# DFTs with real and imaginary parts on the two halves of the partitions, in a kernel that hides them under a selective scan

## The chip, the cores and the metric

The kernel runs on one core of a Trainium2 chip. The core has five engines that run side by side: TensorE (PE, matrix products; its weight loads are listed apart as PEld), VectorE (DVE), ScalarE (ACT), GpSimd (POOL) and SyncE (SP, which issues the DMAs here). The metric is device time in microseconds (us), lower is better. A run is one execution; times before and after are medians of runs.

## The reference, cut to what matters

The input is `x`, four images of 64 x 64 pixels with 96 channels, in float32. Four layers follow one another for each image:

1. A group normalisation and a selective-scan block ("L0": projection, 3 x 3 depthwise convolution, scan in four directions over 4096 tokens, layer norm, gate, output projection), added to `x`. The result is `x0`.
2. A second selective-scan block ("L1") between two Fourier transforms. This is the layer that the change is in:

```
xf  = rfft2(x, axes=(1, 2), norm='ortho')          # 64 x 33 complex values per channel
x1  = stack([xf.real, xf.imag]) -> (64, 33, 192)   # the block works on 192 real channels
att = ss2d(x1)                                     # scan in four directions over 2112 tokens
out = x + irfft2(att[..., 0] + 1j * att[..., 1], s=(64, 64), norm='ortho')
```

3. and 4. Twice linear attention and a feed-forward net with values rounded to 8 bits, on 4096 tokens.

The transforms are small matrix products. Over the width, 64 real values give 33 complex ones; over the height, 64 complex values give 64 complex ones. A complex product over the height is `Re = C*re + S*im`, `Im = C*im - S*re`, so each output sums over a real and an imaginary input.

## The kernel before, in words

**The scan sets the frame.** `scans` (from line 473) runs 1728 steps in order. A step is one group of 4 of the 16 state values, for 128 channels, over one segment of 512, 384 or 320 tokens. Its core is four scans on VectorE (`hx`, `hy`, line 643) and one product on VectorE (`hcy`, line 807, once in each step), with TensorE transposing the inputs into PSUM (line 613) and the outputs back (line 665), ScalarE computing exponentials (line 618), and GpSimd two products (lines 636 and 789). Steps 0 to 767 are the scan of L0 (two phases of 384, two images each). Steps 768 to 1727 are the scan of L1 (four phases of 240, one image each).

**Everything else is side work, cut into pieces.** `fourier`, `project`, `gate`, `gated`, `inverse` and `tokens` are Python generators. Each `yield` ends a piece. A step has three places where at most one piece is put (`slot`, line 723). A place first adds `rate / 3` to an account `due`, and if `due` is 1 or more, a piece is written there and 1 is taken off:

```
due = min(due + st.z.ph.rate / 3, 3.0)
if due >= 1.0:
    due -= E.step(kind)
```

`RATES` (line 26) has one rate per phase: 1.75, 2.3, and four times 2.47 pieces per step. The order on TensorE, VectorE, ScalarE and GpSimd is exactly the order in which the program writes its instructions (`manual_schedule`, line 703), so a piece's matmuls stand between two groups of the scan's transposes and delay those behind them. The DMAs on SP are ordered by the framework's scheduler. A piece that evacuates PSUM can be put off to the next piece (`E.defer`). Within the scan, side work has one PSUM bank (tag `ms`), so a piece that wants the bank waits for the copy out of it.

**The order of the side work.** In phase 1 (steps 384 to 767): the end of L0 for the first pair, then `begin1` for images 0 and 1. `begin1` is `fourier`, then `project` and `gate`. In phase 2: the end of L0 for the second pair, `begin1` for images 2 and 3. Then `end1` for images 0, 1 and 2: `gated` (norm, gate and output projection), `inverse`, `tokens`. What is left when the steps are over runs at once (`E.finish`, line 813). After that `end1` of image 3 runs with nothing beside it, with eight PSUM banks: the tail.

**`fourier` (line 926)** works per image in two stages. The first is over the width: for each of 96 channels, weights `xw[:, :, i]` (64 partitions of width, 64 columns of height, read with a stride of 12 values) and moving operand `fw` (64 x 66: 33 real and 33 imaginary outputs) give `pz` (64 partitions x 66); six channels make a piece and a copy into `z` (line 956). The second is over the height: for each of the 33 frequencies two accumulating matmuls (lines 964 and 965), weights 64 x 96, moving 64 x 128, into `pfx`. By its yields it has 2 + 16 + 17 + 1 = 36 pieces.

**`inverse` (line 981)** also has two stages, for three groups of 32 channels. The first, over the height: for each channel two accumulating matmuls (lines 1001 and 1002), weights `a[:, :, r, i]` (64 partitions x 33 columns, read with a stride of 64 values), moving `ih[:, r]` (64 x 128), into `piv` (33 partitions x 128). Four channels fill a bank, and ScalarE copies it into `v` (line 1005). The second, over the width: for each block of 16 rows of the image two accumulating matmuls (line 1015), weights 33 x 64, moving 33 x 512, into `pio`; VectorE adds the image's `x` (line 1020), and SP stores it. By its yields it has 3 x (2 + 16 + 8) + 1 = 79 pieces.

A float32 matmul appears in the profile as two weight loads and two matmul records. "Record" below means one of these.

## Time and profile before

| what | value |
|---|---|
| median of 3 runs | 12443.53 us (12440.8 to 12446.42) |
| the profiled execution's own time | 12459.57 us |
| its span, first to last instruction | 12457.8 us |
| busy share PE / DVE / ACT / POOL | 79% / 85% / 73% / 71% |
| mean granted TensorE clock | 0.855 |
| steps 384 to 767 (two `fourier`) | 2857.6 to 5533.5 us |
| steps 768 to 1007 (two `fourier`) | 5533.5 to 7073.9 us |
| steps 1008 to 1247 / 1248 to 1487 / 1488 to 1727 | to 8586.9 / 10266.4 / 11891.2 us |
| the three `inverse` beside the scan, first to last matmul | 8227.0 to 8451.3, 9614.5 to 9877.4, 11019.6 to 11269.2 us |
| `inverse` in the tail | 12109.0 to 12235.1 us |

The stretches of the steps are read from the ends of the 1728 executions of line 807. A busy share is an average over stages that have different limits, so the table's shares say little about the transforms; the stretches in which they run have to be read on their own. A "granted clock" of 1.0 is TensorE at full speed, 0.5 at half.

### The profile page before, as it was taken

What the parts mean: (1) busy time and instruction counts of PE and PEld (TensorE: products, weight loads), DVE (VectorE), ACT (ScalarE), POOL (GpSimd) and SP (SyncE); (2) the same over time, 40 slices, a digit from 0 to 9 for tenths busy, and PEclk for the clock granted to TensorE, in tenths of its full rate; (3) what the DMA queues carried; (4) which work ended last, traced back from release to release, by engine and by line L of the source; (5) the groups of instructions that cost most, each with busy time, mean ns of one, the idle gap of its engine ahead of it and who ended that gap; (6) DMA issues with size and microseconds to landing.
All of it is one profiled execution on the core that took longest, in us unless ns stands there. A gap on an engine that the chain in (4) does not pass through costs nothing. (4 is left out here: it accounts for less than half of the span.)

```text
span 12457.8 us, 164218 instructions
## 1 busy us (share of the span) xinstructions
PE 9802.9 (79%) x54392; PEld 6990.4 (56%) x54392; DVE 10588.5 (85%) x10207; ACT 9116.3 (73%) x18615; POOL 8861.4 (71%) x7061
## 2 busy tenths in 40 slices
PE   6677777787788878878888787897778977887766
PEld 3455555456666556556665655665555555665544
DVE  6899999899889989988888889978988699888933
ACT  3678888897778888886677777767776577767723
POOL 2888898887778888886677788866667466675610
PEclk8789999888889989988789899888888688887875
DMA  4454444555554454455443534542244322532231
GB/s 143 119 135 120 116 119 114 145 155 151 143 129 125 119 136 130 118 153 145 136 113 114 137 113 133 150 107 93 76 132 118 80 87 79 155 102 83 82 87 25
DMA packets 1269534, 1468.97 MB, mean 118 GB/s; under 512 B 495491, under 2 KB 1032911, under 8 KB 1259207
## 3 DMA queue, kind: packets, MB, share of 16 engines
q1 hardware_dynamic: 1268679, 1458.47, 42.7%
q8 instruction: 427, 7.00, 0.2%
q14 instruction: 428, 3.51, 0.1%
HBM read 1221.67 MB, written 236.50 MB: 117 GB/s over the span
## 5 line engine op out<-in xcount | busy, mean ns | idle before, releaser
L636 POOL TENSOR_TENSOR hy_l<-du_l,bc_l 128x512 f32<-128x512 f32 (+2 forms) x3456 | 3955.3, 1165 | 2487.9 <-DVE hcy_l L807 1256.0
L789 POOL TENSOR_TENSOR hcx_l<-hx_l,bc_l 128x1024 f32<-128x1024 f32 (+2 forms) x1619 | 3527.7, 2179 | 331.8 <-DVE hx_l L643 285.7
L593 ACT ACTIVATE bx_l<-dut_l,bt_l 128x192 f32<-128x192 f32 (+2 forms) x6272 | 2772.0, 498 | 0.1
L665 PE MATMUL acc_l<-ident,hcy_l 128*128 128x128 f32 (+1 forms) x12012 | 1855.4, 303 | 400.5 <-DVE hcy_l L807 397.0
L665 PE MATMUL acc_l<-ident,hcx_l 128*128 128x128 f32 (+1 forms) x12018 | 1899.0, 307 | 330.2 <-POOL hcx_l L789 326.2
L618 ACT ACTIVATE ax_l<-delta_l,l_alog 128x512 f32<-128x512 f32 (+2 forms) x3456 | 2139.2, 667 | 0.0
L665 PEld LDWEIGHTS acc_l<-ident,hcy_l 128*128 128x128 f32 (+1 forms) x12012 | 1547.3, 155 | 968.1 <-DVE hcy_l L807 586.3
L643 DVE TENSOR_TENSOR_SCAN hx_l<-ax_l,state_l,b_l 128x512 f32<-128x512 f32 (+2 forms) x1653 | 1790.7, 1123 | 277.7 <-PE b_l L613 186.1
L665 PEld LDWEIGHTS acc_l<-ident,hcx_l 128*128 128x128 f32 (+1 forms) x12018 | 1557.5, 157 | 819.2 <-POOL hcx_l L789 577.2
L807 DVE TENSOR_TENSOR hcy_l<-hy_l,bc_l 128x1024 f32<-128x1024 f32 (+2 forms) x1618 | 1950.5, 1205 | 43.2
L643 DVE TENSOR_TENSOR_SCAN hy_l<-b_l,state_l,hy_l 128x512 f32<-128x512 f32 (+2 forms) x1653 | 1793.3, 1119 | 135.0 <-ACT b_l L618 114.5
L618 ACT ACTIVATE b_l<-delta_l,l_alog 128x512 f32<-128x512 f32 (+2 forms) x1917 | 1202.9, 628 | 876.7 <-DVE hx_l L643 831.4
L613 PE MATMUL b_l<-ident,bx_l 128*128 128x128 f32 (+1 forms) x6733 | 1207.2, 309 | 382.9 <-DVE hy_l L643 186.8
L618 ACT ACTIVATE ab_l<-delta_l,l_alog 128x512 f32<-128x512 f32 x1321 | 909.1, 688 | 687.2 <-DVE hx_l L643 655.6
L613 PEld LDWEIGHTS b_l<-ident,bx_l 128*128 128x128 f32 (+1 forms) x6733 | 851.0, 156 | 891.4 <-DVE hy_l L643 283.1
L643 DVE TENSOR_TENSOR_SCAN hx_l<-ax_l,state_l,ab_l 128x512 f32<-128x512 f32 x962 | 1177.0, 1264 | 132.5 <-PE ab_l L613 85.6
L643 DVE TENSOR_TENSOR_SCAN hy_l<-ab_l,state_l,hy_l 128x512 f32<-128x512 f32 x961 | 1176.2, 1258 | 98.1 <-ACT ab_l L618 63.7
L613 PE MATMUL ab_l<-ident,bx_l 128*128 128x128 f32 x5288 | 901.3, 306 | 436.0 <-DVE hy_l L643 219.7
L613 PEld LDWEIGHTS ab_l<-ident,bx_l 128*128 128x128 f32 x5288 | 655.1, 155 | 786.1 <-DVE hy_l L643 294.1
L656 POOL COPY state_l<-hx_l 128x2 f32<-128x2 f32 x1344 | 1077.6, 802 | 0.0
L272 PE MATMUL pc_l<-pad_l,l_dg 128*128 128x512 f32 (+2 forms) x1656 | 796.4, 569 | 80.1 <-ACT uh_l L250 71.8
L176 PE MATMUL pi_l<-xi_l,l_wi 96*128 96x384 f32 (+6 forms) x912 | 467.3, 628 | 266.3 <-DMA xi_l<-xn 97.8
(196 smaller groups left out, 12661.2 us busy)
## 6 DMA issues: line engine op xcount, KB each, us to landing
bc_l<-l_xd_l SPq DMA_DIRECT2D x1536, 256.0 KB
bc_l<-l_xd_l SPq DMA_DIRECT2D x384, 512.0 KB
bc_l<-l_xd_l SPq DMA_DIRECT2D x384, 384.0 KB
us_l<-l_u SPq DMA_DIRECT2D x96, 768.0 KB
l_y<-y_l SPq DMA_DIRECT2D x288, 256.0 KB
bc_l<-l_xd_l SPq DMA_DIRECT2D x192, 320.0 KB
yt_l<-l_y SPq DMA_DIRECT2D x264, 192.0 KB
yt_l<-l_y SPq DMA_DIRECT2D x128, 384.0 KB
```

The lines of the kernel that those rows point to most:

```text
L176: self.nc.tensor.matmul(out[i * cfg.PI : (i + 1) * cfg.PI, :n], wi[:, ki, half, :], xin[:, max(i, ki), :n], start=(ki == 0), stop=(ki == c ...
L272: nc.tensor.matmul(pc[:, : n * 64].rearrange("p (r w) -> p r w", w=64), diag[:, t, :], pad[:, r - p0 + dy : r - p0 + dy + n, dx : dx + 64] ...
L593: nc.scalar.activation(t[:n, b, :, ch], z.dut[:n, b, :, ch], AF.Copy, scale=z.bt[:n, b, m : m + 1])
L613: nc.tensor.transpose(pb[:, t : t + n], st.z.bx[st.q, j][:n, b, st.c], ident[:n, :n])
L618: nc.scalar.activation(out, z.delta[:, st.c, : z.S], AF.Exp, scale=z.blk.A[:, st.c, z.k, n : n + 1])
L636: nc.gpsimd.tensor_tensor(st.hy[:, j, :S], st.z.du[:, st.c, :S], st.z.b[st.q][:, j, :S], ALU.mult)
L643: nc.vector.tensor_tensor_scan(h[:, j, : z.S][:, ::step], a[:, : z.S][:, ::step], b[:, : z.S][:, ::step], 0.0 if z.first else z.state[st.c ...
L656: copy(z.state[st.c][:, n0 : n0 + 2].rearrange("p (j o) -> p j o", o=1), h[:, :, e : e + 1])
L665: nc.tensor.matmul(z.acc[st.c][:n, b, :], hc[:, j, t : t + n], ident, start=(n0 + j == 0 and b == 0), stop=(n0 + j == NST - 1 and b == 0), ...
L789: nc.gpsimd.tensor_tensor(hcx[:, :, :S], hx[:, :, :S], z.c[q][0][:, :, :S], ALU.mult)
L807: nc.vector.tensor_tensor(hcy[:, :, :S], st.hy[:, :, :S], z.c[q][1][:, :, :S], ALU.mult)
```

## The change

In `fourier`, `fw` and `fh` are laid out anew: real outputs of the first stage land on partitions 0 to 63 of `pz`, imaginary ones on 64 to 127. For that each channel has two matmuls (real, imaginary) with the same weights and 33 moving columns each, in place of one with 66. The copy takes 12 channels at once. The second stage then sums over 128 partitions in one matmul per frequency. In `inverse`, the real and imaginary parts of the attention output are loaded onto the two halves of the partitions, padded from 33 to 64 columns with zeros (a GpSimd memset), one group of channels ahead (`bufs=2`). The first stage has two matmuls per channel (real and imaginary output, onto the two halves of the partitions of `piv`), which share their weights and have 64 moving columns each; eight channels fill a bank. The second stage has one matmul per block of 16 rows, summing over all 128 partitions; two blocks go to the two halves of the partitions of one bank, and one VectorE instruction adds `x` for both. `fourier` now has 28 pieces and `inverse` 45. The rates go from 2.3 and 2.47 to 2.25 and 2.35. The constants are rearranged to match.

```diff
@@ -23,7 +23,7 @@
 SM = 512
 LATE, BURST = "late", "burst"
-RATES = [1.75, 2.3, 2.47, 2.47, 2.47, 2.47]
+RATES = [1.75, 2.25, 2.35, 2.35, 2.35, 2.35]
 EXP_LN = "natural_log_exp_and_others"
@@ -926,16 +926,17 @@
 def fourier(E, cst, x, b, dram, out):
     nc = E.nc
     xf = dram.tile([CH, 2, WF * HH], F32, name=f"xf_{b}", tag="xf", bufs=NB)
     out["xf"] = xf
     G = 12
     with E.pool(f"ff{b}") as sp:
-        fw = sp.tile([WW, 2 * WF], F32, name=f"fw_{b}", tag="fw")
+        fw = sp.tile([WW, 2, WF], F32, name=f"fw_{b}", tag="fw")
         nc.sync.dma_start(out=fw, in_=cst["fw"])
-        fh = sp.tile([HH, 2, 2 * HH], F32, name=f"fh_{b}", tag="fh")
+        fh = sp.tile([2 * HH, 2 * HH], F32, name=f"fh_{b}", tag="fh")
         nc.sync.dma_start(out=fh, in_=cst["fh"])
-        z = sp.tile([HH, 2 * WF, CH], F32, name=f"z_{b}", tag="z")
+        z = sp.tile([2 * HH, WF, CH], F32, name=f"z_{b}", tag="z")
         def load(c0):
             t = sp.tile([WW, HH, G], F32, name=f"xw_{b}_{c0}", tag="xw", bufs=2)
@@ -947,24 +948,24 @@
         yield
         for c0 in range(0, CH, G):
             xw, nxt = nxt, load(c0 + G) if c0 + G < CH else None
-            for i0 in range(0, G, 6):
-                pz = E.psum(f"pfz_{b}_{c0}_{i0}")[:HH, : 12 * WF].rearrange("p (c k) -> p c k", c=6)
-                for i in range(6):
-                    nc.tensor.matmul(pz[:, i, :], xw[:, :, i0 + i], fw, start=True, stop=True)
-                c1 = c0 + i0
-                E.defer(
-                    lambda c1=c1, pz=pz: nc.scalar.copy(z[:, :, c1 : c1 + 6], pz.rearrange("p c k -> p k c"))
-                )
-                yield
+            pz = E.psum(f"pfz_{b}_{c0}")[:, : G * WF].rearrange("p (c k) -> p c k", c=G)
+            for i in range(G):
+                for r in range(2):
+                    nc.tensor.matmul(
+                        pz[r * HH : (r + 1) * HH, i, :], xw[:, :, i], fw[:, r, :], start=True, stop=True
+                    )
+                if i == G // 2 - 1:
+                    yield
+            E.defer(
+                lambda c0=c0, pz=pz: nc.scalar.copy(z[:, :, c0 : c0 + G], pz.rearrange("p c k -> p k c"))
+            )
+            yield
         for k0 in range(0, WF, 4):
             nk = min(4, WF - k0)
             px = E.psum(f"pfx_{b}_{k0}").rearrange("p (k r h) -> p k r h", k=4, r=2)
             for i in range(nk):
                 o = px[:CH, i, :, :].rearrange("p r h -> p (r h)")
-                nc.tensor.matmul(o, z[:, k0 + i, :], fh[:, 0, :], start=True, stop=False)
-                nc.tensor.matmul(o, z[:, WF + k0 + i, :], fh[:, 1, :], start=False, stop=True)
-                if i == 1 and nk > 2:
-                    yield
+                nc.tensor.matmul(o, z[:, k0 + i, :], fh, start=True, stop=True)
             def put(k0=k0, nk=nk, px=px):
                 xo = sp.tile([CH, 2, 4, HH], F32, name=f"xo_{b}_{k0}", tag="xo", bufs=2)
@@ -980,47 +981,57 @@
 def inverse(E, cst, att, x, b, x1):
     nc = E.nc
-    G = 32
+    G, HC, WP = 32, 16, 64
+    xs, xd = (t.rearrange("(h w) c -> w h c", w=WW) for t in (x, x1))
     with E.pool(f"fi{b}") as sp:
-        ih = sp.tile([HH, 2, 2 * HH], F32, name=f"ih_{b}", tag="ih")
+        ih = sp.tile([2 * HH, 2, HH], F32, name=f"ih_{b}", tag="ih")
         nc.sync.dma_start(out=ih, in_=cst["ih"])
-        iw = sp.tile([WF, 2, WW], F32, name=f"iw_{b}", tag="iw")
+        iw = sp.tile([2 * WP, WW], F32, name=f"iw_{b}", tag="iw")
         nc.sync.dma_start(out=iw, in_=cst["iw"])
+        def load(c0):
+            a = sp.tile([2 * HH, WP, G], F32, name=f"at_{b}_{c0}", tag="at", bufs=2)
+            nc.gpsimd.memset(a[:, WF:, :], 0.0)
+            for r in range(2):
+                nc.sync.dma_start(
+                    out=a[r * HH : (r + 1) * HH, :WF, :], in_=att[:, :, r * CH + c0 : r * CH + c0 + G]
+                )
+            return a
+        nxt = load(0)
+        yield
+        yield
         for c0 in range(0, CH, G):
-            a = sp.tile([HH, WF, 2, G], F32, name=f"at_{b}_{c0}", tag="at")
-            for r in range(2):
-                nc.sync.dma_start(out=a[:, :, r, :], in_=att[:, :, r * CH + c0 : r * CH + c0 + G])
-            yield
-            yield
-            v = sp.tile([WF, G, 2, HH], F32, name=f"v_{b}_{c0}", tag="v")
-            for i0 in range(0, G, 4):
-                pv = E.psum(f"piv_{b}_{c0}_{i0}").rearrange("p (c r h) -> p c r h", c=4, r=2)
-                for i in range(4):
-                    o = pv[:WF, i, :, :].rearrange("p r h -> p (r h)")
-                    nc.tensor.matmul(o, a[:, :, 0, i0 + i], ih[:, 0, :], start=True, stop=False)
-                    nc.tensor.matmul(o, a[:, :, 1, i0 + i], ih[:, 1, :], start=False, stop=True)
-                    if i == 1:
+            a, nxt = nxt, load(c0 + G) if c0 + G < CH else None
+            v = sp.tile([2 * WP, G, HH], F32, name=f"v_{b}_{c0}", tag="v")
+            for i0 in range(0, G, 8):
+                pv = E.psum(f"piv_{b}_{c0}_{i0}").rearrange("p (c h) -> p c h", c=8)
+                for i in range(8):
+                    for r in range(2):
+                        nc.tensor.matmul(
+                            pv[r * WP : (r + 1) * WP, i, :], a[:, :, i0 + i], ih[:, r, :], start=True, stop=True
+                        )
+                    if i == 3:
                         yield
-                E.defer(lambda i0=i0, pv=pv, v=v: nc.scalar.copy(v[:, i0 : i0 + 4], pv[:WF]))
+                E.defer(lambda i0=i0, pv=pv, v=v: nc.scalar.copy(v[:, i0 : i0 + 8], pv))
                 yield
-            HC = 16
-            for h0 in range(0, HH, HC):
-                xr = sp.tile([WW, HC, G], F32, name=f"xr1_{b}_{c0}_{h0}", tag="xr", bufs=2)
-                nc.sync.dma_start(
-                    out=xr, in_=x.rearrange("(h w) c -> w h c", w=WW)[:, h0 : h0 + HC, c0 : c0 + G]
-                )
-                po = E.psum(f"pio_{b}_{c0}_{h0}").rearrange("p (h c) -> p h c", h=HC)[:WW]
-                for r in range(2):
-                    nc.tensor.matmul(
-                        po, iw[:, r, :], v[:, :, r, h0 : h0 + HC].rearrange("p c h -> p h c"),
-                        start=(r == 0), stop=(r == 1),
-                    )
-                    yield
+            for h0 in range(0, HH, 2 * HC):
+                xr = sp.tile([2 * WW, HC, G], F32, name=f"xr1_{b}_{c0}_{h0}", tag="xr", bufs=2)
+                po = E.psum(f"pio_{b}_{c0}_{h0}").rearrange("p (h c) -> p h c", h=HC)
+                halves = [
+                    (slice(k * WW, (k + 1) * WW), slice(h0 + k * HC, h0 + (k + 1) * HC)) for k in range(2)
+                ]
+                for p, h in halves:
+                    nc.sync.dma_start(out=xr[p], in_=xs[:, h, c0 : c0 + G])
+                for p, h in halves:
+                    nc.tensor.matmul(po[p], iw, v[:, :, h].rearrange("p c h -> p h c"), start=True, stop=True)
+                    yield
+                yield
                 nc.vector.tensor_tensor(xr, xr, po, ALU.add)
-                nc.sync.dma_start(
-                    out=x1.rearrange("(h w) c -> w h c", w=WW)[:, h0 : h0 + HC, c0 : c0 + G], in_=xr
-                )
+                for p, h in halves:
+                    nc.sync.dma_start(out=xd[:, h, c0 : c0 + G], in_=xr[p])
         yield
@@ -1292,10 +1303,10 @@
         "ident": np.eye(128),
         "group": (g[:, None] // 3 == g[None, :] // 3) / 3.0,
         "head_mask": (g[:, None] // 16 == g[None, :] // 16) * 16**-0.5,
-        "fw": np.concatenate([cw, -sw], 1) * rw,
-        "fh": np.stack([np.concatenate([ch, -sh], 1), np.concatenate([sh, ch], 1)], 1) * rh,
-        "ih": np.stack([np.concatenate([ch, sh], 1), np.concatenate([-sh, ch], 1)], 1) * rh,
-        "iw": np.stack([cw.T * fold, -sw.T * fold], 1) * rw,
+        "fw": np.stack([cw, -sw], 1) * rw,
+        "fh": np.block([[ch, -sh], [sh, ch]]) * rh,
+        "ih": np.stack([np.concatenate([ch, -sh]), np.concatenate([sh, ch])], 1) * rh,
+        "iw": np.concatenate([v for m in (cw, -sw) for v in (m.T * fold * rw, np.zeros((WW - WF, WW)))]),
     }
     return {k: np.ascontiguousarray(v, np.float32) for k, v in c.items()}
```

## The prediction

> **What bounds the kernel now.** I read the page first. No engine is full over the whole span, and the chain that ended last changes hands all the time, so the averages decide nothing.
>
> ```profile
> PE 9802.9 (79%) x54392; PEld 6990.4 (56%) x54392; DVE 10588.5 (85%) x10207; ACT 9116.3 (73%) x18615; POOL 8861.4 (71%) x7061
> PE 16%; ACT 12%; DVE 11%; issue 4%; POOL 3%; DMA 2%; SPq 0%; DVEq 0%; POOLq 0%; ACTq 0%
> ```
>
> So I took the stretches in which the transforms run: two of the four `fourier`, the three `inverse` beside the scan, the tail's `inverse`, and what lies between the last step and the tail.
>
> ```profile
> core 0: us, PE busy (x) PEld busy (x) DVE busy (x) ACT busy (x) POOL busy (x), PEclk, DMA share, GB/s
> 3702.00:3812.00 110.00, 101.24 (x706) 87.44 (x705) 92.54 (x76) 89.13 (x195) 82.04 (x60) 0.92 0.58 119
> 6233.00:6347.00 114.00, 112.22 (x671) 93.15 (x672) 83.06 (x70) 74.88 (x132) 66.93 (x44) 0.76 0.44 95
> 8227.00:8451.00 224.00, 220.02 (x1100) 138.29 (x1100) 163.99 (x167) 145.56 (x288) 138.63 (x128) 0.80 0.40 100
> 9614.00:9877.00 263.00, 258.55 (x1050) 152.27 (x1050) 140.47 (x165) 129.22 (x276) 115.58 (x113) 0.64 0.29 69
> 11020.00:11269.00 249.00, 233.44 (x1231) 152.23 (x1230) 193.65 (x171) 158.49 (x294) 167.90 (x126) 0.82 0.38 100
> 12103.00:12237.00 134.00, 124.06 (x432) 75.40 (x432) 8.16 (x13) 13.88 (x24) 0.15 (x1) 0.51 0.25 37
> 11891.00:11921.00 30.00, 14.64 (x79) 8.72 (x80) 12.12 (x23) 7.77 (x14) 0.00 (x0) 0.56 0.40 110
> ```
>
> Here TensorE is the bound: busy 98, 98 and 94% in the three `inverse` stretches, while VectorE falls to 73, 53 and 78%. Line 807 runs 93 times in them, so a step takes 736/93 = 7.9 us, where VectorE needs 498/93 = 5.4. In the tail TensorE is all there is, at half clock. How fast its records go, from the timelines and the chain:
>
> ```profile
> 12108.99 3.60 PE L1001 MATMUL piv<-ih,at 64*33 64x128 f32 x16 [6.65 <-DMA at<-att]
> 12137.15 13.99 PE pio L1015 x16
> 4624.79 1.69 PEld L953 LDWEIGHTS pfz<-fw,xw 64*64 64x64 f32 x12 [5.30 <-issue]
> 67.55 2.03 PE L176 MATMUL pi_l<-xi_l,l_wi 96*64 96x448 f32 x8
> 70.64 0.23 PEld L176 LDWEIGHTS pi_l<-xi_l,l_wi 96*64 96x64 f32 x4 [0.70 <-ACT pad_l L234]
> ```
>
> - First stage of `inverse`, half clock: (3.60 - 0.41)/15 = 0.213 us from one 128-column record to the next (0.41 is one record's mean), so 0.107 at full clock.
> - Second stage: (13.99 - 1.04)/15 = 0.863 per 512-column record. Beside the scan 48 such records take 46.1 to 46.5 us at clock 0.64 to 0.82, so the clock isn't what holds them; I take it to be the stride of the moving operand, which the change keeps.
> - `fourier`, first stage: twelve weight loads of 64 strided columns without a gap, (1.69 - 0.23)/11 = 0.133 each. They, not the 66 columns that follow, set the pace.
> - `project` in the prologue already writes to both halves of the partitions. Eight records of 448 columns take 2.03 us, (2.03 - 0.54)/7 = 0.21 each, where 448 columns alone need 448/128 x 0.107 = 0.37. Two halves run at once. Four loads fit into 0.23, less than twice one load's 0.13, so loads overlap too.
>
> **What the Trainium skill says.** "TensorE: Matmul & The Clock Gate", section "Part 3: Packing small matmuls — row/col tiling": products that land in distinct column groups run concurrently (three of them at 32 columns: 2.38x). The prologue agrees. The same section says that weight loads overlap running matmuls only where the row group differs. Here both halves use the same rows, but the four loads in 0.23 us speak against reading it strictly. Its section "LDWEIGHTS (loading the stationary operand)" gives columns/1.2 ns, 53 ns for 64; the strided loads measure 133, and that counts. "TensorEngine Tiling (Array Packing)", section "Key Properties", says that changing the tiling mode drains TensorE; no run here prices it, and the kernel before changes it as often.
>
> **The change part by part.** Let p be the effective distance between weight loads of 64 strided columns. Fully overlapped it is 0.133/2 = 0.067, not overlapped 0.133. No row shows strided loads that overlap, so p is the unknown.
>
> 1. *`inverse`, first stage.* Before: 384 records, by their own rows 57, 74, 54 us beside the scan and 82 in the tail. After: again 192 matmuls, 384 records, now with 64 moving columns (0.053 to 0.107 each, below the load). So 384 p = 26 to 51 us.
> 2. *`inverse`, second stage.* 48 records at 0.863 = 41 us become 24: 21 us one after another, 10 with both halves at once.
> 3. *`fourier`, first stage.* 192 records at 0.133 = 26 us become 384 with the same loads: 26 to 51 us. This part can lose: each load now serves 33 columns and is made twice.
> 4. *`fourier`, second stage.* 132 records become 66: its row has 19.3 us per image, so -10.
> 5. *Evacuation.* Copies of `piv` 24 x 0.58 to 12 (-7 us of ACT per image), of `pz` 16 x 0.49 to 8 (-4), adds of `x` 12 x 0.68 to 6 (-4 of DVE). In these stretches TensorE covers them: nothing.
> 6. *DMAs.* As many as before: 2 constants, 6 loads of `at`, 12 of `x`, 12 stores. `at` loads one group ahead, which removes waits on `at` within `inverse` (the row above shows 6.65 us at its start, which stays). Nothing to -4 per image.
> 7. *Memset, 128 x 992 on POOL, three per image.* Nearest rows: 128 x 32 in 0.15 us, a product of 128 x 512 in 1.27. So 0.2 to 2.5 us each; behind it queue the products for the scan. POOL is 44 to 67% busy there, which covers it; without cover 9 x 2.5 = 23 us. I take 0.
> 8. *Pieces and rates.* 36 to 28 and 79 to 45. `end1` falls from 449 pieces to 415. Before, the last step ends at 11891.2 and 21 pieces of image 2's `tokens` are still to do. They hold the tail's first matmuls:
>
> ```profile
> 11896.45 0.36 SPq L367 DMA_DIRECT2D yt_l<-l_y  x1
> 11918.80 0.93 PEld L1173 LDWEIGHTS <-h 128*128 128x128 fp8e5 x12 [3.80 <-DVE h L1168]
> 11920.51 1.36 PEld L394 LDWEIGHTS py_l<-ut_l,l_skip 128*128 128x128 f32 x6 [0.78 <-ACT y L1181]
> ```
>
> The order of instructions in the changed kernel puts image 2's last addition before the last steps of the scan. The first loads are issued at 11896.45 and the rest by 11898.8; with about 2 us to land, the tail can start at 11901 and not 11920.5. I take -18, since those pieces now cost something under the scan.
>
> *The tail.* Per group of channels after: first stage 128 p = 8.5, wait for the copy 1.2, second stage 4 x 0.863 = 3.4, together 13. SP then has 4 loads, 4 stores and 2 loads of `at` per group, some 0.6 to 1 us each: about as long. Three groups 40, the start 6, some 5 for DMA: 51 us for 133. **-80** with overlap; with p = 0.133 and the second stage serial, 6 + 3 x 25 + 1 = 82: -51.
>
> *Beside the scan.* Overlapped, an `inverse` needs 36 us of TensorE for an average of 62 + 46 (its rows): -72, for three -216. Not all of it is time. VectorE's 5.4 us per step, with its own gaps some 5.8, lets the stretches shrink from 736 to about 540 at most, and slots that become free are filled with other pieces. I count 0.55: **-120**. Serial, it needs 72: -36 each, -60 at the same share. `fourier`: overlapped -10 per image, of which I count 0.3, since VectorE is 73 to 84% busy there: **-12** in all. Serial it is +15 each; a loss on the bound engine is hidden less, so 0.65 of it: +40.
>
> Sum: -80 - 18 - 120 - 12 = **-230** on the execution's own 12459.6, so 12230. The median of the runs stands 16 below that execution; in the same ratio I get **12215**.
>
> **The rivals.**
>
> - *Strided loads don't overlap (p = 0.133).* The sentence on row groups and the doubled loads speak for it, the four loads in 0.23 us against. -51 - 18 - 60 + 40 = -89: 12355.
> - *Slower: a load of 64 strided columns over 128 partitions costs more than over 64, or mixing halves serialises loads and matmuls.* There are 8 x 384 = 3072 such records. Against 4 x 26 + 57 + 74 + 54 + 82 = 371 us of first stages before, and fixed gains of 18, 4 x 20 and 4 x 10, the account at full price is 3072 p - 509: even at p = 0.166, beyond +25 us at 0.174. That asks for a third more than the 0.133 seen and no overlap. At p = 0.2 it gives +105: 12550. For it: no row shows such a load on 128 partitions. Against: before, a first-stage record of `inverse` at clock 0.80 took 57/384 = 0.15 us with its load of 33 strided columns hidden behind it.
> - *Hidden anyway: the gain in TensorE's time turns into waits elsewhere under the scan,* because SP or the single PSUM bank for side work holds `inverse`. The tail and the 18 us are left, and `fourier` at nothing: -98, 12346. Against: TensorE at 94 to 98% in those stretches.
>
> **How the numbers follow.** Overlap 0.60 (12120 to 12300, by the share counted beside the scan, 0.3 to 1). Not overlapped, or only partly, 0.17; hidden 0.09; both lie at 12300 to 12420. Within 0.2% (about 25 us, what a measurement of this kernel can tell from no change) 0.07; slower 0.07. The range 12130 to 12420 leaves out the last two and a little below. Chances: faster 0.86, same 0.07, slower 0.07.
>
> **What would show it.** In the tail, `inverse` shrinks from 133 us to about 51, with records of its first stage 0.067 apart on average; at 0.133 the first rival holds. In `fourier`, the two matmuls of a channel start nearly together. The tail's first matmul follows the last step by about 10 us, not 29. Beside the scan, `inverse` takes some 19 steps of 6.4 us in place of 31 of 7.9, with VectorE above 80%. I am wrong if the first stage's records lie more than 0.17 apart, if the clock falls in `fourier` for lack of moving columns, so that the scan's own transposes slow down, or if SP becomes what the tail waits for.

## The result, and the profile after

The changed kernel takes 12109.16 us (median of 4 runs, 12101.73 to 12119.34) against 12442.17 for the kernel before (4 runs, 12435.25 to 12446.42). The ratio is 0.9733, with a 95% interval of 0.9717 to 0.975: 333 us saved. The forecast was 12215, with a range from 12130 to 12420. The sign and the likeliest mechanism were right. The gain was 106 us larger than forecast and the time lies below the range.

The profiled execution of the changed kernel took 12108.82 us, with a span of 12106.9 and a mean granted clock of 0.870 (before: 0.855). The page's first line of busy times, and the first line of its chain of work:

```profile
PE 9441.0 (78%) x54800; PEld 6783.4 (56%) x54800; DVE 10572.7 (87%) x10183; ACT 9071.5 (75%) x18534; POOL 8900.0 (74%) x7074
ACT 12%; DVE 12%; PE 11%; issue 3%; POOL 3%; DMA 2%; SPq 0%; DVEq 0%; POOLq 0%; ACTq 0%
```

TensorE is busy 362 us less than before. In the chain its share of the span fell from 16% to 11%, and VectorE's rose from 11% to 12%; the shares add up to only 48% of the span before and 43% after, since the chain doesn't reach back to the start, so this is a hint and no more. The averages say which engine was relieved, not where. For that, here are the stretches that answer to those of the forecast: the same two `fourier`, the three `inverse` beside the scan, the tail's `inverse`, and what lies between the last step and the tail's first matmul.

```profile
core 0: us, PE busy (x) PEld busy (x) DVE busy (x) ACT busy (x) POOL busy (x), PEclk, DMA share, GB/s
3686.80:3775.20 88.40, 82.09 (x741) 72.88 (x741) 68.47 (x57) 67.70 (x147) 62.70 (x46) 0.86 0.62 115
6217.50:6312.50 95.00, 91.27 (x724) 80.20 (x725) 64.35 (x54) 56.37 (x99) 49.77 (x34) 0.68 0.48 103
8240.40:8347.00 106.60, 102.46 (x771) 68.20 (x771) 88.66 (x90) 78.73 (x158) 79.19 (x70) 0.96 0.57 132
9529.00:9639.00 110.00, 104.69 (x763) 69.19 (x764) 83.40 (x95) 71.55 (x152) 70.24 (x69) 0.96 0.50 110
10783.80:10905.00 121.20, 115.70 (x877) 81.32 (x878) 108.64 (x93) 88.48 (x152) 89.32 (x62) 0.97 0.54 124
11841.00:11885.40 44.40, 35.13 (x408) 26.16 (x408) 4.11 (x7) 7.05 (x12) 1.08 (x2) 0.88 0.81 98
11647.20:11660.00 12.80, 3.42 (x17) 3.05 (x16) 0.00 (x0) 0.59 (x1) 0.00 (x0) 0.50 0.60 174
```

Read the length and the clock of each line together. The tail's `inverse` went from 134 us to 44, and its clock from 0.51 to 0.88. The three `inverse` beside the scan went from 224, 263 and 249 us to 107, 110 and 121, and their clock from 0.80, 0.64 and 0.82 to 0.96 or 0.97. Line 807 runs 51 times in them, where it ran 93 times, so a step takes 337.8/51 = 6.6 us instead of 7.9. The two `fourier` stretches are the exception: their clock fell, from 0.92 to 0.86 and from 0.76 to 0.68. Next, the timelines of the changed kernel (start, duration, engine, line, tiles, count, idle time before):

```profile
3686.76 1.80 PE L954 MATMUL pfz<-fw,xw 64*64 64x33 f32 x24
8256.20 1.22 PE L1013 MATMUL piv<-ih,at 128*64 128x64 f32 x16
8259.04 1.88 PE L1029 MATMUL pio<-v,iw 128*64 128x512 f32 x2
11653.01 0.36 SPq L367 DMA_DIRECT2D yt_l<-l_y  x1
11659.19 1.62 PE L394 MATMUL py_l<-ut_l,l_skip 128*128 128x128 f32 x6 [9.38 <-DMA ut_l<-l_u]
11847.50 8.27 PE L1013 MATMUL piv<-ih,at 128*64 128x64 f32 x128 [9.67 <-DMA at<-att]
11856.44 3.67 PE L1029 MATMUL pio<-v,iw 128*64 128x512 f32 x8 [0.68 <-ACT v L1018]
```

First-stage records of `inverse`, each with its own load of 64 strided columns, now start 62 ns apart on average (mean distance of the starts, beside the scan and in the tail); those of `fourier` 66. Two halves do run at once, with their loads. Line 1029 is the second stage. In the tail, 8 records of 512 columns take 3.67 us: four pairs at about 0.87 each, both halves at once. Beside the scan it is different. A `yield` follows each half's matmul, so the two halves fall into different places of a step, with the scan's transposes between them, and the two records of one half take 1.88 us, one after the other. The 24 records of an image come to 22.9 us beside the scan and to 11.0 in the tail. The tail's first matmul (line 394) comes 12.0 us after the last step instead of 29.3.

The time by stretches of steps, in us, read from the ends of line 807 in the profiled executions; the last two columns are the time from the last step to the end of the span, and the median of the runs. The rates are those of the second phase and of the four later ones.

| kernel | rates | 384-767 | 768-1007 | 1008-1247 | 1248-1487 | 1488-1727 | after the last step | median |
|---|---|---|---|---|---|---|---|---|
| before | 2.3/2.47 | 2675.9 | 1540.4 | 1513.0 | 1679.5 | 1624.8 | 566.6 | 12442.2 |
| changed | 2.25/2.35 | 2631.8 | 1526.0 | 1494.0 | 1581.6 | 1561.0 | 459.8 | 12109.2 |
| changed, old rates | 2.3/2.47 | 2669.5 | 1565.9 | 1508.0 | 1584.1 | 1533.6 | 461.7 | 12196.1 |
| only `inverse` changed | 2.3/2.47 | 2678.8 | 1540.3 | 1501.8 | 1590.8 | 1542.5 | 465.7 | 12176.0 |
| only `fourier` changed | 2.3/2.47 | 2672.3 | 1559.9 | 1561.8 | 1612.3 | 1595.5 | 550.4 | 12433.4 |
| before, new rates | 2.25/2.35 | 2651.3 | 1521.6 | 1480.2 | 1641.5 | 1619.6 | 685.6 | 12458.4 |
| `inverse` changed, new rates | 2.25/2.35 | 2637.7 | 1527.0 | 1455.8 | 1574.5 | 1559.9 | 473.6 | 12080.6 |
| changed, slower still | 2.2/2.3 | 2635.3 | 1497.2 | 1464.8 | 1582.7 | 1565.8 | 487.6 | 12098.4 |

From the end of step 0 to that of step 383, all of them take 2626.8 to 2631.9 us. The lower lines are the experiments. Each stretch comes from one execution. How far such a number can be trusted is seen where two kernels place the same pieces in the same steps: the changed kernel and a later one ("second phase only", below) take 2631.8 and 2618.7 us for steps 384 to 767, 13 apart. Differences of that size say nothing.

### The profile page after: what moved, and what is told of

Read it like the earlier page. It is cut to its first block, busy times and chain, and to the rows that moved or that the text cites. A ratio compares the mean times of both kernels' runs of the same rounds, so it can differ in the third digit from the quotient of the medians.

```text
span 12106.9 us, 164888 instructions
## 1 busy us (share of the span) xinstructions
PE 9441.0 (78%) x54800; PEld 6783.4 (56%) x54800; DVE 10572.7 (87%) x10183; ACT 9071.5 (75%) x18534; POOL 8900.0 (74%) x7074
## 5 line engine op out<-in xcount | busy, mean ns | idle before, releaser
L613 PEld LDWEIGHTS b_l<-ident,bx_l 128*128 128x128 f32 (+1 forms) x6718 | 825.8, 152 | 905.8 <-DVE hy_l L643 296.7
L656 POOL COPY state_l<-hx_l 128x2 f32<-128x2 f32 x1344 | 1114.3, 829 | 0.0
```

Of the source, the lines that this page charges most:

```text
L613: nc.tensor.transpose(pb[:, t : t + n], st.z.bx[st.q, j][:n, b, st.c], ident[:n, :n])
L656: copy(z.state[st.c][:, n0 : n0 + 2].rearrange("p (j o) -> p j o", o=1), h[:, :, e : e + 1])
```

## The experiments

Three explanations of the extra gain stood against each other at first: `inverse` is worth more than its 218 us (120 beside the scan, 98 around the tail); `fourier` is worth more than 12; or the lower rates act by themselves, which the forecast had counted at nothing but the pieces left over. The first four kernels take the change apart.

**The change without its rates.**

```diff
-RATES = [1.75, 2.25, 2.35, 2.35, 2.35, 2.35]
+RATES = [1.75, 2.3, 2.47, 2.47, 2.47, 2.47]
```

> The changed kernel with the rates of before (2.3 and 2.47 pieces per step). The side work then ends at step 1688 of 1728 in place of 1722. Theory A (the gain is TensorE time and clock, the rates only fit the pieces into the phases): within 20 us of the changed kernel, 12090 to 12130. Rival B (the surplus over the prediction comes from the slower rates, which thin out all side work): some 60 us or more above it, 12170 or more.

Measured: 12196.11 us, ratio to before 0.9805 (0.9788 to 0.9823). The new rates are worth 87 us of the 333. (The two profiled executions are 70 apart; the one with the old rates stands 17 below its median.) With the old ones the kernel lands within 20 us of the forecast.

**Only `inverse`.** The kernel before, old rates, with the new `inverse` and its constants; `fourier` stays at 66 moving columns and two accumulating matmuls.

```diff
 # against the changed kernel
-RATES = [1.75, 2.25, 2.35, 2.35, 2.35, 2.35]
+RATES = [1.75, 2.3, 2.47, 2.47, 2.47, 2.47]
-            pz = E.psum(f"pfz_{b}_{c0}")[:, : G * WF].rearrange("p (c k) -> p c k", c=G)
...
+                    nc.tensor.matmul(pz[:, i, :], xw[:, :, i0 + i], fw, start=True, stop=True)
```

> Only the new inverse, with the old fourier and the old rates. Theory A: it holds nearly all, the tail's 107 us and 160 to 180 beside the scan: 12150 to 12190. If the new fourier holds the 58 us that steps 384 to 1007 lost, this stands about 55 us above the changed kernel: 12165. Rival B (rates): 12220 or more.

Measured: 12176.02 us, 0.979 (0.9775 to 0.9806), so -263. In the table, 101 of the 283 that its profiled execution gains lie after the last step, and 182 in steps 1008 to 1727, in which the three `inverse` run.

**Only `fourier`.** The kernel before, old rates, with the new `fourier` and its constants.

> Only the new fourier, with the old inverse and the old rates. By the prediction's own account (overlap, 12 us in all, and some 15 because fewer pieces are left over at the end): 12415. If the 58 us between steps 384 and 1007 are fourier's: 12370. If its doubled weight loads cost time, 12450 or more.

Measured: 12433.4 us (12 runs, 12406.59 to 12450.49), 0.9991 (0.9982 to 1.0001): -6, which can't be told from nothing. Added to the new `inverse` at the old rates it stands 20 higher (12196.11 against 12176.02), but the intervals of the two overlap (0.9788 to 0.9823, 0.9775 to 0.9806). So it brought none of the extra gain; that it costs something there is not shown.

**Halves one after another.** The forecast rests on two halves running at once, with their loads. In this variant of the changed kernel, each piece of a first stage has first all matmuls to the lower half of the partitions, then all to the upper half: groups of 6 in `fourier`, of 4 in `inverse`. Records, loads, pieces and rates are the same. The diff shows `fourier`; `inverse` is grouped likewise.

```diff
-            for i in range(G):
+            for i0 in range(0, G, G // 2):
                 for r in range(2):
...
+                    for i in range(i0, i0 + G // 2):
...
```

> The changed kernel, but in each piece of the two first stages all matmuls for the first half of the partitions come first, then all for the second (6 and 6 in fourier, 4 and 4 in inverse); same instructions, same results. Theory A1 (two halves run at once because neighbours in the queue go to different halves): the overlap is lost but at the change of halves, p goes from 0.06 to 0.11 to 0.13, the tail's inverse from 37 to 55 us, the whole 60 to 120 us above the changed kernel: 12170 to 12230. Theory A2 (TensorE looks far enough ahead to pair them whatever their order): within 20 us of it.

Measured: 12231.06 us, 0.9827 (0.9811 to 0.9844), 122 more than the changed kernel. The timelines of this kernel, in `fourier` and in the tail:

```profile
3685.56 2.90 PE L955 MATMUL pfz<-fw,xw 64*64 64x33 f32 x24
11962.15 9.05 PE L1015 MATMUL piv<-ih,at 128*64 128x64 f32 x128 [9.52 <-DMA at<-att]
```

The same 24 records as in line 954 above take 2.90 us instead of 1.80. The four `fourier` stretches hold the same 44 steps and take 461 us instead of 362: 99 of the 122 us. Of these 99, 71 are the first-stage records themselves (186.6 us instead of 116.0); the rest goes with a lower clock in these stretches, 0.63 to 0.72 instead of 0.68 to 0.89. So the overlap of the two halves, loads included, is what the new first stages live on, and records of different halves have to be neighbours for it. How close they have to be isn't a fixed number: groups of 4 in the tail's run of 128 records come to 68 ns a record, almost the 62 of strict alternation; the same groups in the scan's runs of 16 come to 91, and the groups of 6 in `fourier` to 113.

**Which half of the change makes `inverse` fast?** This kernel keeps the first stage of `inverse` on 128 partitions, with one matmul per channel that sums over both parts, but gives up the halves on the output side: 33 columns loaded, 128 moving columns, no padding. The second stage is the old one, two matmuls over 33 partitions for one block at a time. `fourier` is the old one, the rates and the numbers of pieces are those of the new `inverse` with new rates, which is its partner.

```diff
 # against its partner
-                for i in range(8):
-                    for r in range(2):
-                        nc.tensor.matmul(
-                            pv[r * WP : (r + 1) * WP, i, :], a[:, :, i0 + i], ih[:, r, :], start=True, stop=True
-                        )
+                for i in range(4):
+                    nc.tensor.matmul(pv[:WF, i, :, :], a[:, :, i0 + i], ih, start=True, stop=True)
...
```

> As inverse_new_rates (12081), but the new inverse without the two halves of the outputs: the first stage sums over 128 partitions in one matmul per channel (33 columns of weights, 128 moving), the second stage is the old one, with two matmuls of 33 partitions. Same pieces in the same steps. If the clock rises because 128 partitions are in use: first-stage records 0.107 us apart in the tail, its inverse 21 + 41 + 6 = 68 us. If the clock needs the columns too: 0.213 apart, 88 us. Beside the scan the second stage takes 46 us in place of some 25: with the halves worth what TensorE time they save, 30 us in the tail and some 40 to 60 beside the scan, 12150 to 12175. If the sum over 128 partitions is nearly all of the gain: 12110.

Measured: 12240.09 us, 0.9836 (0.982 to 0.9853), against 12080.55 of its partner. What it gives up, the halves on the output side and with them the second stage's sum over 128 partitions, is worth 160 us. That is more than the 70 to 95 that a count of TensorE's time alone had led to expect. Its timeline in the tail, then the stretches of its `inverse` beside the scan and in the tail, and last two of its partner's, the second `inverse` beside the scan and the tail's:

```profile
11938.68 9.51 PE L1010 MATMUL piv<-ih,at 128*33 128x128 f32 x64 [9.54 <-DMA at<-att]
11948.86 13.94 PE L1018 MATMUL pio<-v,iw 33*64 33x512 f32 x16 [0.67 <-ACT v L1011]
```

```profile
8297.60:8455.90 158.30, 150.37 (x691) 88.96 (x692) 109.74 (x96) 95.76 (x177) 89.55 (x65) 0.80 0.40 99
9610.20:9757.80 147.60, 146.95 (x604) 77.25 (x605) 77.78 (x100) 80.11 (x166) 57.88 (x61) 0.74 0.36 76
10920.20:11080.60 160.40, 150.75 (x713) 92.02 (x714) 115.39 (x101) 97.48 (x178) 95.07 (x74) 0.78 0.38 94
11938.70:12010.70 72.00, 69.99 (x240) 33.44 (x240) 7.47 (x11) 13.91 (x24) 0.00 (x0) 0.71 0.38 53
```

```profile
9569.10:9679.70 110.60, 110.20 (x766) 69.22 (x767) 73.99 (x95) 72.98 (x153) 60.13 (x62) 0.94 0.49 100
11819.60:11856.50 36.90, 34.84 (x408) 25.89 (x408) 3.44 (x5) 7.05 (x12) 0.93 (x1) 0.93 0.75 96
```

The second stage is untouched there: 13.94 us for 16 records, the 0.86 each of before. And the clock stays at 0.71 to 0.80, where the partner's four stretches have 0.93 to 0.99.

**Why is `inverse` worth 182 us in the steps and not 120?** A part of the 182 doesn't lie beside `inverse` at all. Its three runs beside the scan have 102 pieces fewer. Where only `inverse` is changed, the pieces therefore end at step 1695 and the last 32 steps have none beside them; before, pieces ran to the last step and 21 were left over. These 32 steps take 190.6 us instead of 236.4 (from the ends of line 807): 46 of the 182. The other 136 lie in steps 1008 to 1695, and they are close to the 120.

Behind these 136 the profiles show more than fewer and denser records: the scan's own transposes share those stretches. Line 665's matmuls in the three stretches, first of the kernel before, then of the changed one (busy time and count, clock):

```profile
8227.00:8451.30 224.30, 70.09 (x401) 0.80 0.40 100
9614.50:9877.40 262.90, 79.91 (x373) 0.64 0.29 68
11019.60:11269.20 249.60, 79.73 (x487) 0.82 0.38 100
```

```profile
8240.40:8347.00 106.60, 31.71 (x218) 0.96 0.57 132
9529.00:9639.00 110.00, 31.07 (x211) 0.96 0.50 110
10783.80:10905.00 121.20, 40.59 (x289) 0.97 0.54 124
```

A record takes 229.73/1261 = 182 ns before and 103.36/718 = 144 after. Take the time in which `inverse` records run away from TensorE's busy time (325.1 of 713.3 us before, 158.5 of 322.9 after), and a step's share is 388/93 = 4.2 us before and 164/51 = 3.2 after. So TensorE gained 325 - 158 = 167 us by fewer and denser records, and about 93 x 0.95 = 88 because everything else in a step took less of TensorE. Of the 0.95 us, the scan's transposes have 0.68: line 665 has 0.44 and line 613 has 0.24 (122.85 us in 93 steps before, 55.19 in 51 after). That sum, 255, is an account of two profiles and not a run of its own, and 136 us of it arrived as time. That the clock rises with the halves is shown by the run above; that the clock is why the transposes ran faster is read from the two numbers side by side.

**Do the rates act phase by phase?** Two kernels give the changed kernel one of the two new rates each, and one the middle between old and new.

```diff
+RATES = [1.75, 2.25, 2.47, 2.47, 2.47, 2.47]    # second phase only
+RATES = [1.75, 2.3, 2.35, 2.35, 2.35, 2.35]     # later phases only
+RATES = [1.75, 2.275, 2.41, 2.41, 2.41, 2.41]   # between
```

> The changed kernel with the new rate in phase 1 (2.25) and the old one (2.47) from phase 2 on. The profiles with old and new rates differ by 38 us in phase 1 and by 40 in phase 2, and by 14, 2 and -27 in the phases after. If each phase's rate acts by itself: 12196 - 38 = 12158. If the gain is a matter of where the pieces happen to fall, any value between 12109 and 12196.

> The changed kernel with the old rate in phase 1 (2.3) and the new one (2.35) from phase 2 on. From step 768 on the pieces fall into the same steps as in the changed kernel. If each phase's rate acts by itself: 12109 + 38 = 12147. If the 38 us of phase 1 are paid back or doubled later: more than 20 us away from that.

> The changed kernel with rates half way between old and new (2.275 and 2.41). Theory C1 (a slower rate is cheaper piece by piece, since fewer steps carry three pieces): half the gain, about 12152. Theory C2 (what counts is which pieces meet which steps, and the new rates happen to fall well): no order; as far as 40 us from 12152 on either side.

Measured: 12136.81 (0.9762, 0.9746 to 0.9779), 12149.92 (0.9771, 0.9756 to 0.9785) and 12172.71 us (0.9787, 0.9773 to 0.9802). From 12196.11, the second phase's rate gains 59 and the later one 46, together 105 where both at once gained 87: within the spread of the runs, they act by themselves. In the profiled executions, too, the first leaves steps 768 to 1007 at 1563.1 us and shortens steps 384 to 767 to 2618.7; the second does the reverse (2679.5, and 1525.9). Half the change gains 23 of 87 by its median; its interval overlaps with that of the old rates (0.9788 to 0.9823).

**Are the rates worth the same without the change?** The kernel before, with the new rates, and the kernel with only `inverse` changed, with the new rates:

> The kernel before with the new rates alone. Some 100 pieces of tokens are then left when the steps end and run alone, about 150 to 200 us. Theory C (the slower rates make the steps cheaper whatever the transforms are): phase 1 (steps 384 to 767) falls from 2676 to about 2638 us and phase 2 from 1540 to about 1527, as in inverse_new_rates; the whole ends at 12450 to 12550. Theory G (they pay only with the new inverse): phases 1 and 2 as before, 2670 and 1540.

> The new inverse with the old fourier, as inverse_alone, but at the new rates. The old fourier has 8 pieces more per image, so about 15 pieces are left over when the steps end, which cost some 20 us there. Theory C (the rates alone bring the 87 us, the new fourier nothing): 12176 - 87 + 20 = 12110. Theory D (the slower rates pay only with the new fourier's fewer pieces): 12165 or more.

Measured: 12458.4 us for the first (18 runs; 1.0015, 1.0006 to 1.0024), slightly slower than before. The table shows why: its steps are 122 us shorter, and the part after the last step is 119 longer, since 104 pieces are left when the steps are over, in place of 21. The changed kernel has no piece left over. So in the old kernel, lower rates only move 83 pieces from the steps to the time after them, at no gain. What lets the changed kernel have lower rates without pieces left over is their smaller number: in the scan `fourier` has 4 x 8 fewer and `inverse` 3 x 34, together 134.

The second kernel takes 12080.55 us (12075.44 to 12096.01; 0.9717, 0.9703 to 0.9732). Its median is the lowest of all: 29 us below the whole change, with the old `fourier` and 16 pieces left over. But its interval overlaps with that of the whole change (0.9717 to 0.975), and changed kernels further below come to 0.971 and 0.9712. So the new `fourier` isn't needed for the gain; that the kernel is faster without it isn't shown. At a neighbouring rate the low time is gone:

```diff
 # against this kernel
-RATES = [1.75, 2.25, 2.35, 2.35, 2.35, 2.35]
+RATES = [1.75, 2.26, 2.37, 2.37, 2.37, 2.37]
```

> As inverse_new_rates, with rates 2.26 and 2.37, so that some 8 pieces are left over at the end and not 16. If the leftover pieces are what counts: 12070. If slower is better whatever is left: 12085 to 12100.

Measured: 12142.84 us, 0.9762 (0.9742 to 0.9783). Neither reading expected this. Less than one per cent more in the rates costs 62 us, 30 of them in steps 1008 to 1247 alone (1485.7 instead of 1455.8).

**Does the clock hold `fourier` back?** The changed `fourier` moves 33 columns per load, where it moved 66. Here each first-stage matmul moves 66 again: the second 33 columns are computed into the place of the next channel, whose own matmul overwrites them (the last channel's go to a spare place). Nothing else differs.

```diff
...
-                        pz[r * HH : (r + 1) * HH, i, :], xw[:, :, i], fw[:, r, :], start=True, stop=True
+                        pz2[r * HH : (r + 1) * HH, i : i + 2, :], xw[:, :, i],
+                        fw[:, r : r + 1, :].to_broadcast([WW, 2, WF]), start=True, stop=True,
```

> The changed kernel, but each matmul of fourier's first stage moves 66 columns in place of 33; the second 33 fall where the next channel's matmul overwrites them. Same results, same number of matmuls and loads, which still set the pace (0.067 us per record with both halves). Theory E (the new fourier is no gain because its short matmuls let the clock fall, to 0.68 to 0.89 in its stretches): the clock rises towards 0.9, and the time falls by 15 to 30 us, to 12080 to 12095. Theory F (the clock isn't the reason; 28 pieces in place of 36 put the same work into fewer steps): 12105 or more.

Measured: 12089.19 us (12073.74 to 12094.84; 0.9712, 0.9697 to 0.9727), 20 below the changed kernel although it does more work; the intervals touch (0.9717 to 0.975). Its timeline, its four `fourier` stretches, and the second and fourth stretch of the changed kernel, which were not shown above:

```profile
3692.47 1.83 PE L955 MATMUL pfz<-fw,xw 64*64 64x66 f32 x24
```

```profile
3692.50:3775.40 82.90, 76.25 (x741) 67.60 (x741) 68.39 (x57) 67.75 (x147) 64.93 (x46) 0.95 0.67 123
4595.30:4683.00 87.70, 80.12 (x744) 70.85 (x745) 67.76 (x57) 65.71 (x141) 65.42 (x46) 0.91 0.61 121
6213.10:6300.10 87.00, 82.37 (x724) 71.61 (x725) 64.31 (x54) 56.38 (x99) 49.84 (x34) 0.81 0.54 113
7013.10:7094.60 81.50, 76.39 (x730) 68.61 (x731) 64.03 (x54) 56.36 (x105) 59.72 (x44) 0.92 0.51 108
```

```profile
4593.90:4680.50 86.60, 80.10 (x744) 71.31 (x745) 67.83 (x57) 65.77 (x142) 65.52 (x46) 0.89 0.65 123
7024.30:7116.00 91.70, 88.17 (x730) 77.64 (x731) 64.54 (x55) 57.60 (x107) 61.71 (x44) 0.72 0.47 97
```

Twice the columns cost 0.03 us per 24 records, so the columns don't set the pace. The clock is 0.95, 0.91, 0.81 and 0.92 where the changed kernel has 0.86, 0.89, 0.68 and 0.72, and the same 44 steps take 339 us instead of 362.

**In order, or by chance?** There are two readings of the rates. Either slower rates help in order (C1), or it is a matter of which piece meets which step (C2), so that the smallest change moves the time either way. Three more kernels:

```diff
+RATES = [1.75, 2.2, 2.3, 2.3, 2.3, 2.3]         # slower
+RATES = [1.75, 2.24, 2.34, 2.34, 2.34, 2.34]    # nudged; and the same with the wide fourier
```

> The changed kernel with rates 2.2 and 2.3 in place of 2.25 and 2.35: about 24 pieces are left when the steps are over, which then run by themselves for some 28 us (before with the same kind of leftover: 104 pieces cost 119 us, 1.15 us each). C1, slower rates help in order: from the old rates to the new ones the steps gained about 25 us for each per cent of rate (87 us for 2.2% and 4.9%, taken at 3.5%), so 2% less gains another 50 in the steps and loses 28 after them: about 12090, and no more than 12115. C2, alignment of pieces with steps: steps anywhere from 60 us shorter to 60 us longer, so 12080 to 12200, and 12150 or more would speak against C1.

> The changed kernel with rates 2.24 and 2.34, half a per cent lower; the side work ends three steps before the last, so nothing is left over. C1: within 10 us of the changed kernel, 12095 to 12110. C2: the same pieces meet other steps, so the time moves by 20 to 60 us in either direction: below 12090 or above 12130.

> As rates_nudged, with fourier's first stage moving 66 columns per matmul, of which the next one overwrites 33 (the extra columns are computed and thrown away). If the gain of 20 us seen at the rates 2.25 and 2.35 is the granted clock in fourier's stretches, it stands here too: 10 to 30 us below rates_nudged, whatever that is. If it was alignment, the two lie within 10 us or the wide one is slower.

Measured: 12098.35 us (12088.1 to 12113.33; 0.972, 0.97 to 0.974), 12098.32 (12091.83 to 12103.04; 0.9715, 0.9699 to 0.9732) and 12092.86 (12082.46 to 12095.99; 0.971, 0.9694 to 0.9726). The nudged kernel lies where C1 put it and not where C2 did; the slower one fits both, and stays below the 12115 that C1 allowed. From 2.25/2.35 downward the time is flat within 11 us: the slower rates gain more in the steps (43 and 48 us against before in steps 768 to 1007 and 1008 to 1247, where the changed kernel has 14 and 19), and give 28 us back after the last step, to pieces left over. Upward it climbs: 12172.71 at 2.275/2.41, 12196.11 at the old rates. The wide `fourier` gains 5 us here and not the 10 to 30 expected; its stretches are 8 us shorter (339 against 348) at a clock of 0.98, 0.91, 0.89 and 0.81 against 0.90, 0.91, 0.74 and 0.77. By what was expected, 5 us within overlapping intervals speaks for the meeting of pieces and steps. So by the medians the clock in these stretches is worth some 20 us at most, and perhaps nothing that the runs can tell.

## Why the prediction was right or wrong

**Steps 1 and 2, `inverse` on TensorE: right in the first stage, and in the second only in the tail.** The unknown p was put at 0.067 us with overlap and 0.133 without. It is 0.062 in `inverse` and 0.066 in `fourier`. With halves that aren't neighbours it rises to 0.091 and 0.113, and the time by 122 us. The second stage was priced at 21 us per image one after another and 10 with both halves at once. It came out at the lower price in the tail (11.0), but at the higher one beside the scan (22.9), where a `yield` parts the halves; the sum counted 10 there. No run puts the two matmuls into one piece. The rival without overlap and the slower rival, which needed more than 0.174, are out. The Trainium skill's "TensorE: Matmul & The Clock Gate", section "Part 3: Packing small matmuls — row/col tiling", has loads overlap running matmuls only where the row group differs. These halves use the same rows, and the measured 62 ns per load and matmul, against the 133 that a load takes by itself, decide against reading it strictly.

**The tail: right, a little more.** Forecast -80 and, for the handover of step 8, -18. Measured: 134 to 44 us and 29.3 to 12.0, together 107 us after the last step (566.6 to 459.8).

**Beside the scan, `inverse`: right in size, in part by luck.** Forecast -120, measured -136 in steps 1008 to 1695 (only `inverse` changed, old rates); in the changed kernel, there are 17 steps of 6.6 us per `inverse`, where 19 of 6.4 were expected. The working counted 0.55 of 216 us. The records gave 167 of the 216: they came to 53 us of TensorE per image and not to 36, 29.8 for the first stage instead of 26, and 22.9 for the second instead of 10. But everything else in those steps took about 88 us less of TensorE while the granted clock was higher, and of that the working had nothing. The two errors go against each other, and the share was a guess. The remaining 46 of the 182 us belong to step 8. The rival that the gain is hidden anyway is out.

**Steps 3 and 4, `fourier`: about right in size, and the named danger was there.** Forecast -12, measured -6 with an interval of -22 to +1 when it is changed alone, and 20 us more, within overlapping intervals, once `inverse` is changed. The stretches shrank from 431.8 to 361.7 us, but hold 44 steps instead of 53, so a step in them takes 8.2 us as before, and the nine others have to run elsewhere. The fall of the clock for lack of moving columns, listed as something that would make the forecast wrong, is there (0.76 to 0.68 for image 2, 0.92 to 0.72 for image 3) and worth some 20 us at most. Step 7 took the memset as covered: it takes 0.92 us each time, inside the 0.2 to 2.5 that were allowed for.

**Step 8, "Pieces and rates": the step that failed.** It counted the 21 pieces left over at -18 and everything else about pieces and rates at nothing. It read the smaller number of pieces as a shorter list to be finished, and not as steps that are freed. At the old rates the freed steps lie at the end: with only `inverse` changed, the last 32 steps have no piece and take 46 us less. At the new rates the pieces spread over nearly all steps instead, and that measures another -87 for the whole kernel. Counted in the order in which the program places its pieces, with old and new rates:

| steps | pieces, old rates | pieces, new rates | time, new less old (us) |
|---|---|---|---|
| 384-767 | 797 | 797 | -38 |
| 768-1007 | 550 | 525 | -40 |
| 1008-1247 | 534 | 519 | -14 |
| 1248-1487 | 518 | 503 | -2.5 |
| 1488-1727 | 440 | 495 | +27 |

From step 768 on, 55 pieces leave the full steps for the end, where 39 steps had none with the old rates and 5 have none with the new ones; they save 56 us and cost 27. Of the five times, -14 is hardly clear of the spread of a stretch, and -2.5 is not. In steps 384 to 767 the pieces are the same and only their spread differs: with the old rate 107 steps have three pieces and 9 have none, with the new one 93 have three and all have some. That even spreading is how the gain comes about is argued from these counts; that the rates do it, phase by phase, is shown. The 46 and the 87 us together are more than the 106 by which the forecast missed; `fourier` takes back a part.

The sum: with the old rates the forecast of 12215 would have stood against 12196. But part of that closeness is luck, errors that cancel: `inverse` at -263 instead of -218, by the 46 us at the end of the steps, and `fourier` at +20 beside it (within the spread) instead of -12. With the rates, 12109.

**What stays open.** Why the steps 1008 to 1247 take 1455.8 us with the old `fourier` at 2.25/2.35 and 1485.7 at 2.26/2.37, and whether half the change of the rates gives half of the gain (12172.71 was measured, 12152 would be half). Both may be a matter of which piece meets which step; no run took that apart.

## What to carry to other kernels

If small matmuls leave half of TensorE's columns empty, put two of them on the two halves as direct neighbours in the program, with nothing that parts them, and count twice: their own time, and the other records in the stretch, which ran faster here as the granted clock rose. When a change makes side work shorter or its pieces fewer, retune the rate at which it is mixed in; here that alone was a quarter of the gain, and in the unchanged kernel the same rates gained nothing. When you price side work, ask also which steps it frees, and what a step without it takes. Check every part alone and together with the others: the `fourier` part of this change brings nothing that the runs can tell.

## What the runs showed of the hardware

- The granted clock doesn't follow how long TensorE is busy. The kernel before is busy 124 of 134 us in the tail, at 0.51; there the first stage alone, its records back to back, has 0.50. The first stage over 128 partitions with 33 columns loaded has 0.75 in the tail. With both halves, the tail's stretch has 0.88, and 0.93 from its first matmul to its last. The Trainium skill's "TensorE: Matmul & The Clock Gate", section "Part 1: The HAM clock gate (the "warmup" mystery)", ties the clock to how busy TensorE has been recently; in these runs it rises with how much of the array works.
- Moving columns count too. Averaged over the four `fourier` stretches, the clock is 0.83 to 0.89 in the six kernels with the old `fourier` (66 moving columns, one half), 0.74 to 0.84 in the eight with the new one in alternation (33 columns per load), and 0.90 in the two with 66 columns per load on both halves, at the same pace. The two have 0.78 and 0.83 without the added columns. Rows and loaded columns were not taken apart.
- Loads of 64 strided columns to one half follow one another every 133 ns, and every 62 to 66 ns when neighbours go to different halves, over the same rows.
- What grouping by halves costs depends on the run: groups of 4 channels pair almost fully in a run of 128 records (68 ns), partly in runs of 16 (91), groups of 6 in runs of 24 hardly (113).
